# Two-layer graph network on one core: rows of A dealt over six attention strips, roots in three parts, Pool's first work in written order

## The chip, the cores and the metric

The kernel runs on one core of a Trainium2 chip. The core has a matrix engine (TensorE, "PE" in the profile; its weight loads are "PEld"), a vector engine (DVE), a scalar engine (ACT), a general engine (POOL) and a queue processor (SP) that mostly starts DMA transfers. Each engine works through its own list of instructions in order; semaphores make one wait for another. The metric is the time of the program on the device in microseconds, the median of several runs.

## The reference

x has 2708 rows (nodes) of 128 features, adj is a 2708 x 2708 matrix A of zeros and ones. Everything is fp32. Layer 0 adds three things to x and normalizes the rows:

```python
deg = clip(adj.sum(axis=1), 1.0)
dis = deg ** -0.5
diffusion = (dis[:, None] * adj * dis[None, :]) @ x - x
norms = maximum(norm(x, axis=-1), 1e-8)
sim = x @ x.T / (norms[:, None] * norms[None, :])
attn = softmax(beta * sim * adj, axis=1)
x = layernorm(x + diffusion + sigmoid(alpha) * (attn @ x - x))
```

Layer 1 multiplies x by a weight matrix, forms an attention from two scores per node, divides it by A times its exponentials, and multiplies by A again; its result is added to x and normalized. The change touches layer 0 only.

## The kernel before, in words

A is never kept whole on the chip. Its transpose is read in strips of 512 columns: six strips (the last has 148 columns), each of 22 blocks of 128 rows. Layer 0 has two stages.

**Attention** goes over the six strips in the order 2, 3, 4, 0, 1, 5; n counts this order from 0, and k counts the 22 blocks of a strip from 0. For each block, TensorE computes the similarities (`sim`, from the normalized and transposed rows `xn_t`, or by transposing a tile `turned` that an earlier strip has stored, since sim is symmetric). DVE multiplies them by a piece of A's transpose and by beta into `p_t` (and copies `sim` into `turned` where a later strip will need it). ACT takes the exponential of `p_t` in place, POOL adds it to `total`, and TensorE multiplies it with the rows of x into `att_acc`. Six buffers hold `p_t`, four PSUM tiles hold `sim`. After a strip, `attended` sums `total` by matmuls (`sums`), copies `att_acc` by ACT (`tr_sb`), transposes it (`tr_ps`) and adds it into `att`; this is written at k = 5 of the next strip. `att` starts as -sigmoid(alpha) * x.

**Preparing** the normalized rows runs within n = 0: squares and their sums (by DVE for the first two parts of the nodes, then by ACT), the power -1/2 on POOL (`norms`, tile `ss`), the scaling (`xn`, by DVE or ACT), and transposes by TensorE whose result is copied into `xn_t` (`turn_rows`, by ACT).

**Degrees**: the sum over a row of A. A block of 128 rows is loaded in two halves (`row`, 677 KB each, two buffers) by SP, and ACT adds each half up (an activation of 1354 columns with an accumulator, written to `deg2`). `roots` adds the halves, clips them and takes the power -1/2 on POOL (`dis`). In n = 5 the rows of x are multiplied by `dis` in place (L582), as soon as the attention has used them.

**Diffusion** (L703) then goes over strips 0 to 5 of A's transpose, loaded whole (`strip`, 5.8 MB in two halves, three homes in memory that pieces, stored tiles and other buffers of the attention must leave first): 22 blocks of two-pass matmuls for each, with the layer norm and the beginning of layer 1 for the strip before in between. `nat` are further loads of A by POOL's queue for layer 1.

**What sets the order.** SP's queue is one list: pieces of A's transpose (`load_piece`, five buffers), rows and strips stand in it one behind another, and a transfer whose buffer isn't free holds all that follow. For nearly all of n = 0, `strict` is set, and each PE, DVE and ACT instruction is pinned behind the one written before it on its engine (`pinned`). After that a planner orders the instructions by its own estimate of costs, within the dependences; a pin only says behind which instruction one must come. In the kernel before, POOL's instructions are not pinned, so that memsets written much later can come first, and the activations on `row` are pinned behind the last pinned ACT instruction only. The degrees are written from n = 1 on; the planner moves the last of them behind the end of n = 5.

The two steps that the change deals with, before it:

```python
if n > 0 and todo and (k % 6 == 5 if m < n else (k - 4 * n) % 3 == 1):
    degree(todo.pop(0))
if n == NS - 2 and k == NB - 1:
    while todo:
        degree(todo.pop(0))
```

Of the kernel before, what the change touches and what calls it, by code (L numbers as in the profile page):

```python
# [9 lines left out]
F32 = mybir.dt.float32  # L10
AF = mybir.ActivationFunctionType
ALU = mybir.AluOpType
AX = mybir.AxisListType
PSUM = bass.MemoryType.PSUM

P = 128
N = 2708
D = 128
NB = (N + P - 1) // P
# [3 lines left out]
NS = (N + SW - 1) // SW  # L23
# [7 lines left out]
Q = 256  # L31
# [8 lines left out]
TINY = 1e-18  # L40
# [4 lines left out]
def grouped(  # L45
# [14 lines left out]
    nc = tc.nc  # L60
# [13 lines left out]
    def blocks(s):  # L74
        return min(SW // P, NB - s * (SW // P))
# [10 lines left out]
    x_sb = lp.tile([P, NB, D], F32, name="x_sb")  # L86
    ident = const.tile([P, P], F32, name="ident")
# [3 lines left out]
    minus_half = const.tile([P, NB], F32, name="minus_half")  # L91
    nc.gpsimd.memset(minus_half, -0.5)
    plus_half = const.tile([P, 1], F32, name="plus_half")
# [10 lines left out]
    sig = const.tile([P, 1], F32, name="sig")  # L104
# [5 lines left out]
    def counted(name, pattern, base, step, size):  # L110
# [7 lines left out]
    node = counted("node", [[P, NB]], 0, 1, NB)  # L118
# [11 lines left out]
    pad = const.tile([P, NB], F32, name="pad")  # L130
    from_n = const.tile([P, NB], F32, name="from_n")
    after_node = const.tile([P, 2], F32, name="after_node")

    row0, row1, rest, head = (
        const.tile([P, 1], F32, name=n) for n in ("row0", "row1", "rest", "head")
    )

    four = const.tile([P, 32], F32, name="four")

    def constants():  # L140
        dve("tensor_scalar", pad, node, N - 0.5, 1e6, ALU.is_gt, ALU.mult)
        dve("tensor_scalar", from_n, node, float(-N), None, ALU.add)
        dve("tensor_scalar", after_node, node[:, 0:2], 1.0, None, ALU.add)
        dve("tensor_scalar", row0, node[:, 0:1], 0.0, None, ALU.is_equal)
        dve("tensor_scalar", row1, node[:, 0:1], 1.0, None, ALU.is_equal)
        dve("tensor_scalar", rest, node[:, 0:1], 1.5, None, ALU.is_gt)

        dve("tensor_scalar", head, node[:, 0:1], 1.5, TINY, ALU.is_lt, ALU.max)
        dve("tensor_reduce", four, ident.rearrange("p (q g) -> p g q", q=4), AX.X, ALU.add)

    deg2 = const.tile([P, NB, 2], F32, name="deg2")
    deg = const.tile([P, NB], F32, name="deg")
    dis = const.tile([P, NB], F32, name="dis")
    live = const.tile([P, NB], F32, name="live")

    cnt = const.tile([P, NS, 2, 2], F32, name="cnt")
    theta = const.tile([P, 2], F32, name="theta")
    ntheta = const.tile([P, 2], F32, name="ntheta")


    latest = {}

    def pinned(engine, op, *args, **kwargs):
        with ExitStack() as e:
            if engine in latest:
                e.enter_context(tc.issue_after(latest[engine].ins))
            latest[engine] = op(*args, **kwargs)  # L167

    strict = []

# [5 lines left out]

    def dve(op, *args, **kwargs):
        if strict:
            pinned("DVE", getattr(nc.vector, op), *args, **kwargs)
        else:  # L180
            getattr(nc.vector, op)(*args, **kwargs)  # L181

    def act(op, *args, **kwargs):
        if strict:
            pinned("ACT", getattr(nc.scalar, op), *args, **kwargs)
        else:
            getattr(nc.scalar, op)(*args, **kwargs)  # L187

    def over(t, m, n):
        return t.unsqueeze(2).to_broadcast([P, m, n])  # L190
# [81 lines left out]
    att = lp.tile([P, NB, D], F32, name="att")  # L272
# [3 lines left out]
    with ExitStack() as es:  # L276
        pa = pool("pa", stack=es)
# [4 lines left out]
        shift = pa.tile([P, 1], F32, name="shift")  # L282
# [40 lines left out]

        def norms(b0, b1):
            r = ss[:, b0:b1]
            nc.gpsimd.tensor_scalar(r, r, 1e-16, None, ALU.max)
            nc.gpsimd.tensor_tensor(r, r, minus_half[:, b0:b1], ALU.pow)

        def normalize(b0, b1):
            dve(  # L330
# [11 lines left out]
        def turn_rows(b0, b1, by):  # L342
            tp = ps_tp.tile([P, SW // P, P], F32, tag="tp", name="xn_ps")
            for b in range(b0, b1):
                mm(nc.tensor.transpose, tp[:, b - b0, :], xn(b, b + 1)[:, 0, :], ident)
            by(
                xn_t[:, b0 * P : b1 * P],
                tp[:, : b1 - b0, :].rearrange("p b i -> p (b i)"),
            )

        def by_act(o, i):
            act("copy", o, i)


        wa = pa.tile([P, 2], F32, name="wa")
        w_t = pa.tile([P, D], F32, name="w_t")
        spread = pa.tile([P, 1], F32, name="spread")
        up = pa.tile([P, 2], F32, name="up")
        down = pa.tile([P, 2], F32, name="down")
# [26 lines left out]
        squares(12, 16)  # L386
        norms(12, 16)

        def bounds():

            dve("tensor_tensor", up, up, down, ALU.subtract)
            nc.gpsimd.tensor_tensor(spread, spread, plus_half, ALU.pow)
            dve("tensor_scalar", spread, spread, 0.55, None, ALU.mult)
            dve("tensor_scalar", theta, up, spread, None, ALU.mult)
            for b, far, op in ((0, -100.0, ALU.is_lt), (1, 100.0, ALU.is_gt)):
                edge = pa.tile([P, 1], F32, name=f"edge{b}")
                lim = 0.5 if b == 0 else Q - 1.5
                dve("tensor_scalar", edge, node[:, b : b + 1], lim, far, op, ALU.mult)
                dve(
                    "tensor_tensor", theta[:, b : b + 1], theta[:, b : b + 1], edge,  # L400
                    ALU.add,
                )
            dve("tensor_scalar", ntheta, theta, -1.0, None, ALU.mult)

        def attention_starts():

            act("activation", sig, sig, AF.Exp, scale=-1.0)
            dve("tensor_scalar", sig, sig, 1.0, None, ALU.add)
            dve("reciprocal", sig, sig)
            dve("tensor_scalar", att, x_sb, sig, -1.0, ALU.mult, ALU.mult)  # L410

        def degree(ib):

            for h in range(2):
                z = pa.tile([P, N // 2], F32, tag="row", name="row", bufs=2)
                nc.sync.dma_start(z, adj[ts(ib, P), h * (N // 2) : (h + 1) * (N // 2)])
                pinned(
                    "ACT", nc.scalar.activation, z, z, AF.Copy,
                    accum_out=deg2[:, ib, h : h + 1],
                )  # L420

        def roots(b0, b1):

            t = deg[:, b0:b1]
            nc.vector.tensor_tensor(t, deg2[:, b0:b1, 0], deg2[:, b0:b1, 1], ALU.add)
            nc.vector.tensor_scalar(live[:, b0:b1], t, 0.0, None, ALU.is_gt)
            nc.vector.tensor_scalar(t, t, 1.0, None, ALU.max)
            nc.gpsimd.tensor_tensor(dis[:, b0:b1], t, minus_half[:, b0:b1], ALU.pow)

        def attended(s, acc, total):  # L430

# [18 lines left out]
        todo = list(range(NB))  # L450
        ended = None
        scaled = set()
        for n, s in enumerate(order):
            v, nb = width(s), blocks(s)
            acc = ps_acc.tile([P, SW], F32, tag="acc", name="att_acc")
            total = lp.tile([P, SW], F32, tag="total", name="total", bufs=2)
            nc.gpsimd.memset(total, 0.0)
            if v < nb * P:
                nc.gpsimd.memset(total[:, v : nb * P], 1.0)
            blocks_j = taken(n)  # L460

            prep = {
                (0, 1): lambda: normalize(12, 16),
                (0, 16): attention_starts,
                (0, 18): bounds,
                (0, 20): constants,
                (2, 14): lambda: roots(0, 6),
                (3, 16): lambda: roots(6, 12),
                (4, 17): lambda: roots(12, 18),
                (5, 2): lambda: roots(18, NB),  # L470
            }
            turns = {
                3: lambda: turn_rows(12, 16, by_act),
                7: lambda: (turn_rows(16, 20, by_act), turn_rows(20, 22, by_act)),
                13: lambda: turn_rows(0, 4, by_act),
                17: lambda: turn_rows(4, 8, by_act),
# [15 lines left out]
            place = {o: m for m, o in enumerate(order)}  # L492
            late_accs = []
            for k, jb in enumerate(blocks_j):
                if (n, k) in prep:
                    prep[n, k]()
                if n == 0 and k in turns:
                    turns[k]()
# [1 line left out]
                m = place[jb // 4]  # L500
# [7 lines left out]
                else:  # L508
# [2 lines left out]
                        xn_t[:, s * SW : s * SW + v], start=True, stop=True,  # L511
                    )
                p_t = pz.tile([P, SW], F32, tag="p", name="p_t")
                dve(
                    "scalar_tensor_tensor", p_t[:, :v], sim[:, :v], gentle,
                    pieces[s, jb // 4][:, jb % 4, :v], ALU.mult, ALU.mult,
                )
# [19 lines left out]
                r = valid(jb)  # L537

                def grown(p_t=p_t, r=r):
                    act("activation", p_t[:, :v], p_t[:, :v], AF.Exp, bias=shift)  # L540
                    nc.gpsimd.tensor_tensor(  # L541
                        total[:r, :v], total[:r, :v], p_t[:r, :v], ALU.add
                    )

                grown()
# [17 lines left out]
                if k == 5 and ended:  # L563
                    attended(*ended)
                    ended = None
                if n > 0 and todo and (k % 6 == 5 if m < n else (k - 4 * n) % 3 == 1):
                    degree(todo.pop(0))
                if n == NS - 2 and k == NB - 1:
                    while todo:
                        degree(todo.pop(0))  # L570
                if n == NS - 1 and k in (7, 13, 18, 21):

                    done = sorted(blocks_j[: k + 1 if k == NB - 1 else k - 1])
# [31 lines left out]
    e2_p = late.tile([P, NB], F32, name="e2_p")  # L605
    e2_w = late.tile([P, NB, 32], F32, name="e2_w")
    ct = late.tile([P, 4], F32, name="ct")
    nc.gpsimd.memset(e2_w, 0.0)
    nc.gpsimd.memset(x1[:, NB - 1, :], 0.0)

    tot = ps_tot.tile([P, 2, SW], F32, name="tot")
    early = KEPT * SW // 4
# [390 lines left out]
    def by_dve(o, i):  # L1003
        dve("tensor_copy", o, i)
# [691 lines left out]
```

## Time and profile before

| what | value |
|---|---|
| median of 3 runs | 762.48 us (762.22 to 765.44) |
| the profiled execution | 763.92 us |
| its span, first to last instruction | 762.0 us |
| busy: PE, DVE, ACT, POOL | 721.7, 453.2, 419.7, 259.1 us |
| start and n = 0 (0 to 60 us): PE busy | 51.41 us |
| 60 to 195 us (n = 1 to n = 4): PE busy | 133.45 of 135 us |
| 222 to 250 us: PE busy, granted clock | 22.75 of 28 us, 0.88 |
| 250 to 345 us (diffusion): PE busy | 95.00 of 95 us |
| row halves: issue to landing, min, median, max | 3.8, 5.8, 13.0 us |

The profile is of one execution. It lists each instruction's start and length, the idle time of its engine before it, and what ended that idle time (the releaser). L167, L175, L181 and L187 are lines of helpers that issue for PE, DVE and ACT, so a group is told by its tiles. The granted clock is the share of TensorE's full clock.

### The profile page before, as it was taken

The numbers are of one execution on the slowest core, as the hardware profiler recorded it, in microseconds if no ns is written. First come the engines' busy times: TensorE is split into PE (matmuls) and PEld (weight loads), VectorE is DVE, ScalarE is ACT, GpSimd is POOL, SyncE is SP. The second block draws the span as 40 slices with busy tenths as digits, with TensorE's granted clock in tenths as the row PEclk, the third lists the DMA queues.
The fourth block names the chain that finished last, engine by engine and source line by source line (L and its number), as shares of the span: only waits on it lengthen the run. The fifth ranks groups of instructions, "written<-read, shape, count | busy, mean of one in ns | idle before, by whom it ended". The sixth has DMA issues, their size and how long they took to land. (4 is left out here: it accounts for less than half of the span.)

```text
span 762.0 us, 7796 instructions
## 1 busy us (share of the span) xinstructions
PE 721.7 (95%) x2561; PEld 350.4 (46%) x2561; DVE 453.2 (59%) x947; ACT 419.7 (55%) x601; POOL 259.1 (34%) x255
## 2 busy tenths in 40 slices
PE   6989999999997999999898799999999999999995
PEld 4434454545553444445334344444444445544444
DVE  4786776664631443235895998998999982203032
ACT  4747777868551222112264599999999994001000
POOL 6857696979741000001124887111111000000000
PEclk9999999999998999999999999999999999999999
DMA  8738988898989996535369835964444430898970
GB/s 299 282 134 317 313 321 310 321 342 302 345 305 412 379 346 240 188 125 208 117 243 241 255 102 187 223 187 158 173 171 143 157 135 1 269 314 301 319 236 22
DMA packets 67522, 179.87 MB, mean 236 GB/s; under 512 B 4238, under 2 KB 18354, under 8 KB 64450
## 3 DMA queue, kind: packets, MB, share of 16 engines
q1 hardware_dynamic: 52996, 123.10, 45.7%
q0 software_dynamic: 8208, 53.30, 22.1%
q10 hardware_dynamic: 6270, 2.90, 1.3%
q8 instruction: 22, 0.36, 0.2%
q14 instruction: 26, 0.21, 0.1%
HBM read 176.44 MB, written 2.84 MB: 235 GB/s over the span
## 5 line engine op out<-in xcount | busy, mean ns | idle before, releaser
L541 POOL TENSOR_TENSOR total<-total,p_t 128x512 f32<-128x512 f32 (+2 forms) x132 | 152.4, 1155 | 44.5 <-ACT p_t L187 28.3
L167 PE MATMUL num<-ring,wt 128*128 128x512 f32 (+1 forms) x288 | 128.3, 545 | 7.5 <-DVE q L167 4.9
L167 PE MATMUL m_acc<-q,xws 128*128 128x512 f32 x240 | 120.5, 592 | 0.4 <-ACT q L167 0.4
L703 PE MATMUL dif_acc<-strip,x_sb 128*128 128x512 f32 (+1 forms) x264 | 107.7, 557 | 5.3 <-DVE x_sb L582 4.6
L181 DVE SCALAR_TENSOR_TENSOR p_t<-sim,gentle,piece 128x512 f32<-128x512 f32 (+1 forms) x111 | 71.3, 670 | 50.2 <-PE sim L175 35.9
L175 PE MATMUL att_acc<-p_t,x_sb 128*128 128x512 f32 (+1 forms) x228 | 97.2, 545 | 3.4 <-ACT p_t L187 3.1
L167 DVE COPY q<-num 128x512 f32<-128x512 f32 x144 | 86.4, 613 | 16.6 <-PE num L167 15.5
L1233 PE MATMUL h_acc<-ring,m_sb 128*128 128x512 f32 x220 | 95.7, 593 | 0.0
L187 ACT ACTIVATE p_t<-p_t,shift 128x512 f32<-128x512 f32 (+1 forms) x111 | 69.4, 656 | 31.4 <-DVE p_t L181 30.8
L167 PEld LDWEIGHTS num<-ring,wt 128*128 128x128 f32 x288 | 51.5, 190 | 67.4 <-issue 55.7
L167 DVE SCALAR_TENSOR_TENSOR q<-sr_b,nc_s,q 128x1536 f32<-128x1536 f32 (+1 forms) x48 | 77.4, 1613 | 1.2 <-ACT q L167 1.2
L167 ACT ACTIVATE q<-q,head,rest 128x1536 f32<-128x1536 f32 (+1 forms) x48 | 70.5, 1509 | 8.5 <-DVE ring L167 4.5
L703 PEld LDWEIGHTS dif_acc<-strip,x_sb 128*128 128x128 f32 x264 | 47.2, 194 | 56.0 <-issue 49.5
L167 PEld LDWEIGHTS m_acc<-q,xws 128*128 128x128 f32 x240 | 45.5, 190 | 57.1 <-issue 55.7
L954 POOL DMA_INDIRECT ring<-in_adj_t,k_no x24 | 33.5, 1397 | 108.0 <-PE num L167 103.1
L167 ACT ACTIVATE row<-row 128x1354 f32<-128x1354 f32 x44 | 58.3, 1324 | 17.6 <-DMA row<-in_adj 17.2
L1233 PEld LDWEIGHTS h_acc<-ring,m_sb 128*128 128x128 f32 x220 | 41.3, 190 | 49.3 <-issue 49.3
L167 ACT ACT_TABLE_LOAD x48 | 61.6, 1283 | 3.8 <-issue 2.9
L167 ACT ACTIVATE q<-q,c_s 128x1536 f32<-128x1536 f32 (+1 forms) x48 | 62.7, 1354 | 0.3
L175 PEld LDWEIGHTS att_acc<-p_t,x_sb 128*128 128x128 f32 x228 | 39.1, 190 | 49.6 <-ACT p_t L187 27.6
L1248 DVE TENSOR_TENSOR hh<-rows,x 128x512 f32<-128x512 f32 (+1 forms) x6 | 3.8, 641 | 85.2 <-PE rows L1171 82.5
L1243 ACT COPY ht<-h_acc 128x512 f32<-128x512 f32 (+1 forms) x6 | 3.2, 536 | 91.3 <-PE h_acc L1233 91.2
(270 smaller groups left out, 823.0 us busy)
## 6 DMA issues: line engine op xcount, KB each, us to landing
row<-in_adj SPq DMA_DIRECT2D x44, 677.0 KB, 5.8
strip<-in_adj_t SPq DMA_DIRECT2D x10, 2816.0 KB, 14.8
ring<-in_adj_t SPq DMA_DIRECT2D x27, 1024.0 KB, 5.0
piece<-in_adj_t SPq DMA_DIRECT2D x24, 1024.0 KB, 6.2
nat<-in_adj_t POOLq DMA_DIRECT2D x22, 768.0 KB
piece<-in_adj_t SPq DMA_DIRECT2D x7, 512.0 KB, 6.0
strip<-in_adj_t SPq DMA_DIRECT2D x2, 814.0 KB, 13.8
last<-in_adj_t POOLq DMA_DIRECT2D x1, 1628.0 KB
```

Of the source, the lines that this page charges most:

```text
L167: latest[engine] = op(*args, **kwargs)
L175: op(*args, **kwargs)
L181: getattr(nc.vector, op)(*args, **kwargs)
L187: getattr(nc.scalar, op)(*args, **kwargs)
L541: nc.gpsimd.tensor_tensor(total[:r, :v], total[:r, :v], p_t[:r, :v], ALU.add)
L703: nc.tensor.matmul(acc[:, :v], x_sb[:, jb, :], st[:, jb, :v], start=(jb == 0), stop=(jb == NB - 1),)
L954: nc.gpsimd.indirect_dma_start(out=ring[g % RING][P - G :, :], out_offset=None, in_=adj_t[:, :], in_offset=bass.IndirectOffsetOnAxis(ap=k_ ...
L1233: nc.tensor.matmul(acc[:, : h1 - h0], m_sb[:, kb + b, :], a[:, b, h0:h1], start=(kb + b == 0), stop=(kb + b == NB - 1),)
L1243: nc.scalar.copy(ht[:, h0:h1], acc[:, : h1 - h0])
L1248: nc.vector.tensor_tensor(hh[:, b0 : b0 + n, :], rows[:, :n, :], x1[:, ib + b0 : ib + b0 + n, :], ALU.add)
```

## The change

- **Degrees.** `rows_at` says at which k of which strip a block of rows is written: three in n = 0, six in n = 1, five in n = 2 and n = 3, three in n = 4, none in n = 5. Each is put in by `in_order`, which pins it behind the last `p_t` of DVE and the last exponential of ACT (`behind`).
- **Roots** come in three parts (blocks 0 to 8, 8 to 18, 18 to 22) instead of four, at n = 3, k = 2; n = 4, k = 1; n = 4, k = 14, and are pinned too. The last part was at n = 5, k = 2.
- **att** is started strip by strip (at k = 14 of n = 0, k = 4 of the others) instead of for all nodes at k = 16 of n = 0; the sigmoid moves to k = 12.
- **bounds and constants**, small DVE work, move from n = 0 into n = 1, in three parts each.
- **Pool** goes through the new helper `gps`, so that its work in n = 0 stands as written, and two memsets of layer 1 (`e2_w`, `x1`) are pinned behind its last pinned instruction.
- **The second part's transposes** (blocks 12 to 16) are copied into `xn_t` by DVE instead of ACT.

The diff, cut:

```diff
-    def constants():
+    def constants(part):
...
+    def gps(op, *args, **kwargs):
+        if strict:
+            pinned("POOL", getattr(nc.gpsimd, op), *args, **kwargs)
         else:
-            getattr(nc.scalar, op)(*args, **kwargs)
+            getattr(nc.gpsimd, op)(*args, **kwargs)
...
+        def by_dve(o, i):
+            dve("tensor_copy", o, i)
...
+        def attention_starts(s):
+            mine = slice(s * 4, s * 4 + blocks(s))
+            dve(
+                "tensor_scalar", att[:, mine, :], x_sb[:, mine, :], sig, -1.0, ALU.mult,
+                ALU.mult,
+            )
+
+        behind = {}
+
+        def in_order(f):
+
+            latest.update(behind)
+            strict.append("some")
+            f()
+            strict.pop()
...
-            nc.gpsimd.memset(total, 0.0)
+            gps("memset", total, 0.0)
...
-                (0, 16): attention_starts,
-                (0, 18): bounds,
-                (0, 20): constants,
-                (2, 14): lambda: roots(0, 6),
-                (3, 16): lambda: roots(6, 12),
-                (4, 17): lambda: roots(12, 18),
-                (5, 2): lambda: roots(18, NB),
+                (0, 12): alpha_starts,
+                (1, 7): lambda: bounds(0),
+                (1, 9): lambda: bounds(1),
+                (1, 11): lambda: bounds(2),
+                (1, 13): lambda: constants(0),
+                (1, 15): lambda: constants(1),
+                (1, 17): lambda: constants(2),
+                (3, 2): lambda: roots(0, 8),
+                (4, 1): lambda: roots(8, 18),
+                (4, 14): lambda: roots(18, NB),
+            }
+
+            rows_at = {
+                0: (13, 16, 19), 1: (5, 8, 11, 14, 17, 20), 2: (4, 9, 12, 15, 18),
+                3: (4, 9, 13, 16, 19), 4: (3, 6, 9), 5: (),
             }
             turns = {
-                3: lambda: turn_rows(12, 16, by_act),
+                3: lambda: turn_rows(12, 16, by_dve),
...
-                if n > 0 and todo and (k % 6 == 5 if m < n else (k - 4 * n) % 3 == 1):
-                    degree(todo.pop(0))
-                if n == NS - 2 and k == NB - 1:
-                    while todo:
-                        degree(todo.pop(0))
+                if n > 0 and (n, k) in prep:
+                    in_order(prep[n, k])
+                if k == (14 if n == 0 else 4):
+                    in_order(lambda: attention_starts(s))
+                if k in rows_at[n]:
+                    in_order(lambda: degree(todo.pop(0)))
...
-    nc.gpsimd.memset(e2_w, 0.0)
-    nc.gpsimd.memset(x1[:, NB - 1, :], 0.0)
+    pinned("POOL", nc.gpsimd.memset, e2_w, 0.0)
+    pinned("POOL", nc.gpsimd.memset, x1[:, NB - 1, :], 0.0)
```

## The prediction

> **What bounds the kernel now.** I read the page's slices first, then TensorE's timeline over the first 250 us, then, wherever TensorE stood, the engine it stood for. TensorE is busy 721.7 of the 762.0 us of the span, so only its idle or slowed time can be won. The change touches the first 230 us. The slices (19 us each):
>
> ```profile
> PE   6989999999997999999898799999999999999995
> PEclk9999999999998999999999999999999999999999
> DMA  8738988898989996535369835964444430898970
> ```
>
> PE's first three digits are the start and strip n=0; the 7 in the thirteenth slice (229 to 248 us) comes with the lowest clock of the page. That place by stretches of 5 us (length; busy time of PE, weight loads, DVE, ACT, POOL; granted clock; DMA share; GB/s):
>
> ```profile
> 225.00:230.00 5.00, 4.33 (x16) 2.17 (x15) 0.92 (x4) 0.00 (x0) 0.00 (x0) 1.00 1.02 419
> 230.00:235.00 5.00, 2.70 (x6) 0.91 (x6) 0.49 (x4) 2.79 (x4) 0.00 (x0) 1.00 1.04 407
> 235.00:240.00 5.00, 2.72 (x3) 1.18 (x4) 1.40 (x3) 0.00 (x0) 2.14 (x3) 0.63 1.05 408
> 240.00:245.00 5.00, 5.00 (x10) 2.13 (x9) 0.00 (x0) 0.00 (x0) 0.00 (x0) 0.69 1.03 425
> ```
>
> The timelines of PE, ACT and POOL say who waited for whom (start, length, engine, line; in brackets the idle time before it and its releaser):
>
> ```profile
> 229.86 2.84 PE L703 MATMUL dif_acc<-strip,x_sb 128*128 128x512 f32 x6 [0.68 <-DMA strip<-in_adj_t]
> 231.71 1.33 ACT L167 ACTIVATE row<-row 128x1354 f32<-128x1354 f32 x1 [8.83 <-DMA row<-in_adj]
> 235.20 1.03 POOL L428 TENSOR_TENSOR dis<-deg,minus_half 128x4 f32<-128x4 f32 x1 [12.58 <-DVE deg L427]
> 237.28 10.86 PE L703 MATMUL dif_acc<-strip,x_sb 128*128 128x512 f32 x18 [4.58 <-DVE x_sb L582]
> ```
>
> The last two row halves of A land at 231.7, so the last degrees, their roots and the scaling of x_sb (L582) are late, and the diffusion of strip 0 stops at its fifteenth block for 4.58 us. SP's timeline shows why they land late: they are issued at 218.35, behind half a strip, on a DMA that is full (share above 1).
>
> ```profile
> 192.60 0.50 SPq L691 DMA_DIRECT2D strip<-in_adj_t  x1
> 215.00 0.46 SPq L691 DMA_DIRECT2D strip<-in_adj_t  x1
> 218.35 2.31 SPq L416 DMA_DIRECT2D row<-in_adj  x2
> 220.84 72.78 SPq L691 DMA_DIRECT2D strip<-in_adj_t  x10
> ```
>
> The stalls of the first strip (timelines of POOL, PE and DVE):
>
> ```profile
> 5.98 0.69 POOL L608 MEMSET e_w<- 128x704 f32 x1
> 17.97 1.35 POOL L327 TENSOR_TENSOR ss<-ss,minus_half 128x6 f32<-128x6 f32 x1
> 17.10 1.13 PE L167 MATMUL sim<-xn_t 128*128 128x512 f32 x2 [1.29 <-ACT xn_t L167]
> 41.26 2.04 DVE L167 TENSOR_SCALAR att<-x_sb,sig 128x2816 f32<-128x2816 f32 x1 [0.37 <-DVE sig L167]
> 45.25 1.12 PE L167 MATMUL sim<-xn_t 128*128 128x512 f32 x2 [1.72 <-ACT xn_t L167]
> ```
>
> **The change part by part.** Sums are against the profiled span, 762.0 us (that execution took 763.92).
>
> *Rows earlier, roots (18, NB) in n=4: the stall goes.* In the built order SP issues the last two row halves before the last two pieces, and ACT takes them after the third and fifth p_t of n=5 (before: after the last). The scaling of the last blocks then waits for nothing but its attention matmuls. Removed from PE's queue: 4.58 us; the 0.68 us for strip 0's second half; and the slow clock. For the clock, 18 matmuls took 10.86 us where full speed takes 18 x 0.43 = 7.7 (0.86 us per pair, as at 222.40: 14 in 6.17): 3.1 us. [...] Together 8.4 us.
>
> *What is late next: the strips.* Strip 0's first half loses its place at 192.6: both halves now stand behind the last piece, whose buffer comes free with the fourth p_t of n=5, about 205 (DVE did those at 203.7 to 205.4). Halves of 2.88 MB at the 0.41 MB/us of the rows above take 7.0 us each, so with 2 us of start-up they land near 214 and 221. Diffusion starts near 220 (below) and needs the second half 11 x 0.86 = 9.5 us later. Strip 1 (5.8 MB), nat (2.4) and strip 5 (1.7) follow until 221 + 9.9 / 0.41 = 245; strip 1, ahead of strip 5 in SP's queue, lands by about 240 and its first half, first needed near 239, by 234 even when shared with nat. Cost 0, with some 5 us of cover. From there PE was 95.00 of 95 us busy (250 to 345), so the gain passes on.
>
> *n=5 without diffusion between its matmuls.* Before, 3.5 us of diffusion (218.1 to 219.9, 220.2 to 221.9) filled PE there; in the new order none, and the row sums (sums, 2 matmuls) stand ahead of diffusion in PE's queue and wait for Pool. Pool in n=5: 22 additions of 0.53 us, and now the root (1.04) and the memsets of e2_w and x1 (0.69 + 0.20) among them: 13.8 us against 14 us of PE work. Pool's idle time of before in n=5 (4.95 us) was ACT's waiting; bounds 0 and 2.5 us of waiting for Pool, I take 1.2. ACT has two row halves there instead of six, which gives back about half of PE's 0.63 + 0.58 us of idle in 195 to 200 and 210 to 215: -0.5. Diffusion's start: attention's end of before, 222.6, less the 3.5, -0.2 (below), -0.5, +1.2, and 0.5 for the sums: 220.1.
>
> *Start: Pool in written order.* The memset of e2_w no longer stands between norm and power: -0.66 us to the first sim. But both memsets of total (0.53 each) now follow the second norm and push the first addition from 12.70 to about 13.0.
>
> *Second part's transposes by DVE.* The copy runs on DVE at 14.0 to 14.7, after the third p_t, instead of ACT at 16.48, and PE's 1.29 us goes: sim of k = 4 at 15.0 instead of 17.1. It does not last: ACT's normalizing of blocks 16 to 21 waits for Pool's power, 17.97 + 1.35 before, and Pool (second power to 12.0, memsets, three additions) reaches its end at about 19.2 again, at best 18.7. So at k = 7 the gain of both edits is -0.5 (bounds 0 and -1.3).
>
> *Three degrees in n=0.* ACT now has two row halves (1.32 + 0.19 us each) after the p_t of k = 13, 16 and 19 (k from 0; before, two near the strip's end). With two row buffers, the second pair is issued when ACT has finished the first: p_t 13 ends at 36.1, the rows at 37.5 and 39.0; issue 37.7, landing 5.8 us later (median of 44; 3.8 to 13.0) at 43.5, less with the DMA share of 0.43 here: 42.8. ACT takes them until 45.8, then copies xn_t, which the sim of k = 18 waits for: 46.3 instead of 45.25, and instead of 42.9 with nothing in the way: a stall of 3.4 us. Queued behind it on ACT are all later p_t, and PE's matmuls behind those. The third pair lands near 49 and 50.5, and ACT is done with it at 53.5; p_t 20 and 21 end at 54.8 and the strip at 56.0. Before it ended at 56.2, since DVE then spent 2.04 us on att, 2.3 on bounds and 1.0 on constants between p_t, and ACT took two row halves at the same place. Net with the start: -0.2 (bounds -1.5 and +3.5). [...]
>
> *att by strips, bounds and constants in n=1, roots in three parts.* The same work in DVE's gaps, 88 us busy of 135 between 60 and 195: 0. Theta's 1.25 us against 0.14 for its neighbours is waiting for Pool; six slices of att could each wait for one addition (1.28), spread over six strips. Cover: PE 133.45 of 135 busy. n=1 to n=4 have 36 row halves on ACT in both orders, a buffer's two uses mostly 4 to 6 p_t apart in both: 0, between -1.5 and +1.5. Spread's power (0.55 on Pool) moves to the end of n=0: 0.
>
> Sum: -8.4 + 1.2 - 0.5 - 0.2 = -7.9 us; span 754.1. On the median shown, 762.48 - 7.9 = 754.6.
>
> **Rivals.** 0.5% is about what a measurement of this kernel can tell from no change: under 758.7 is faster, over 766.3 slower.
> - *Forecast, 754.6* (own range 751.5 to 758.5). For: the chain row, degree, root, x_sb is plain, and nothing after 250 us stands in the way.
> - *The clock falls in n=0, or DVE holds p_t of n=5 for the last degree* (deg now stands among them and waits for ACT's last row half): -7.9 + 3.1 + 1.5 = -3.3, 759.2. [...] Against: the low DMA share shortens the landing.
> - *The stall only changes its place: strip 0 comes late.* If SP is held at the last piece until t, PE waits t + 9 - 220, and the clock falls too: at t = 215.8 the gain is gone, 762.5. Against: nothing but DVE's fourth p_t and ACT's rows of n=4 holds it.
> - *Slower: landing of the rows in n=0.* Each us beyond 5.1 at p_t 16 stops ACT, so PE, and delays the third pair's issue too: about 2 us for one, and 3.1 of clock. At 7.5 us of landing the 7.9 are gone (2 x 2.4 + 3.1), from 9.4 us on it is slower by 0.5%; at 10.5, 2 x 5.4 + 3.1 - 7.9 = +6.0, 768.5. The 13.0 us happened with the DMA full, which it is not here.
>
> **How the numbers follow.** Forecast 0.62, second 0.20, strip 0 late 0.11, slower 0.07. The time is the first's. Leaving out the slower case and part of its neighbour above, and the far end below, the range is 751.0 to 761.5. Faster: 0.62 and some of the second, with 0.1 of it that falls under 758.7: 0.72; same 0.20; slower 0.08.
>
> **What would show it.** Right: no wait of PE for x_sb L582 near 230; the last row on ACT before 213; PE's clock 1.00 from 220 to 250; strip 0's diffusion ending near 239 instead of 247; strips still 22.6 us apart after it. In n=0: the sim of k = 4 near 15.0, a stall before that of k = 18 of 2.5 to 4 us with ACT waiting for row's DMA, and the strip's last attention matmul near 56. Wrong: a clock under 1 at 40 to 55, PE waiting for strip by DMA, or sums waiting for Pool by more than 2.5 us.

## The result, and the profile after

The changed kernel takes 761.1 us (median of 20 runs, 758.39 to 772.14); the kernel before, run beside it, 762.43 (20 runs, 757.36 to 769.06). The ratio is 0.9993, 95% interval 0.9972 to 1.0014: no change that can be measured, where 754.6 was forecast. The profiled execution of the changed kernel was the longest of its 20 (772.14 us); up to the end of diffusion (358.1 us in both) it keeps pace with the profile before. What it has more lies behind that, where the change does nothing; the greater part is one wait of PE for a transfer of layer 1:

```profile
474.21 2.05 PE L173 MATMUL num<-ring,wt 128*128 128x512 f32 x2 [8.82 <-DMA ring<-in_adj_t,k_no]
```

The comparison below is therefore of the first 250 us, and a second trace of the same kernel (e1) stands beside it.

The slices of the page of the changed kernel (19.3 us each):

```profile
PE   8989999999999999999998895999999999999995
PEclk9999999999979999999999997999999999999998
```

The 7 of PE before 250 us is gone. A low digit of the clock has come in the twelfth slice, 212 to 231 us. By stages (busy time of PE, weight loads, DVE, ACT, POOL; granted clock; DMA share; GB/s):

```profile
0.00:60.00 60.00, 53.26 (x146) 27.03 (x147) 34.48 (x61) 37.39 (x89) 37.95 (x49) 0.97 0.81 284
60.00:195.00 135.00, 131.86 (x444) 66.55 (x442) 92.87 (x162) 100.48 (x151) 107.84 (x87) 1.00 0.87 306
195.00:222.00 27.00, 26.61 (x100) 17.06 (x99) 14.06 (x36) 17.12 (x34) 20.45 (x29) 0.81 0.98 331
222.00:250.00 28.00, 26.76 (x86) 13.84 (x85) 6.20 (x19) 4.55 (x9) 5.63 (x10) 1.00 0.97 361
250.00:345.00 95.00, 95.00 (x301) 42.84 (x303) 36.51 (x172) 16.48 (x24) 3.58 (x10) 1.00 0.67 245
```

From 222 to 250 PE is busy for 26.76 us at full clock; before it was 22.75 at 0.88. So the stall at 230 is really gone, and with it the slow clock behind it. But 0 to 60 has fallen from 1.00 to 0.97, and n=5 (195 to 222) from 1.00 to 0.81. Four points of the schedule show the account, each read as the start of ACT's copy of a finished accumulator to tr_sb, in us of the trace:

| kernel | n=0 ends | n=4 ends | n=5 ends | strip 0's diffusion ends |
|---|---|---|---|---|
| before | 56.35 | 202.99 | 222.60 | 247.32 |
| changed | 58.66 | 207.00 | 227.09 | 247.07 |
| changed, second trace (e1) | 59.16 | 206.61 | 223.69 | 246.97 |
| e2, two rows in n=0 | 52.02 | 204.93 | 218.42 | 243.07 |
| e3, wide sums | 57.71 | 205.05 | 221.21 | 240.10 |
| e5, sums behind | 57.97 | 205.10 | 221.87 | 240.75 |
| e6, e2's rows and sums behind | 52.26 | 205.79 | 222.13 | 241.01 |
| e7, before with earlier rows | 56.21 | 205.80 | 224.97 | 246.18 |
| e8, dummies in n=0 | 56.66 | 204.38 | 221.24 | 244.54 |
| e9, e6 with wide sums | 51.98 | 204.20 | 217.84 | 237.70 |

Before, 3.86 us of strip 0's diffusion (1.98 + 1.88) lay inside n=5. With these taken off n=5 and put to the last stretch, the lengths before are 56.35, 146.64, 15.75 and 28.58 us. The changed kernel's are 58.66, 148.34, 20.09 and 19.98. So the last stretch gives 8.6 us, very near the 8.4 costed, and 2.3, 1.7 and 4.3 are lost ahead of it: the gain was made and spent in the same 250 us. (For n=1 to n=4, the 1.7, no run gives a cause.)

**Where the 2.3 of n=0 went.** Timelines of PE and ACT of the changed kernel:

```profile
42.91 1.02 PE L173 MATMUL att_acc<-p_t,x_sb 128*128 128x512 f32 x2
46.99 1.13 PE L173 MATMUL sim<-xn_t 128*128 128x512 f32 x2 [3.06 <-ACT xn_t L173]
47.96 1.81 PE L173 MATMUL att_acc<-p_t,x_sb 128*128 128x512 f32 x2
42.44 1.32 ACT L173 ACTIVATE row<-row 128x1354 f32<-128x1354 f32 x1
45.05 1.33 ACT L173 ACTIVATE row<-row 128x1354 f32<-128x1354 f32 x1 [1.20 <-DMA row<-in_adj]
46.38 0.56 ACT L173 COPY xn_t<-xn_ps 128x512 f32<-128x512 f32 x1
```

ACT waits for the second pair of row halves with the copy of xn_t queued behind them, PE stands 3.06 us, and what follows runs slow (1.81 us where 1.02 is usual). From this sim to the end of n=0 the four traces with one stretch of 3.41 us at half clock here take 11.62 to 11.67 us (the changed kernel, e1, e3, e5); e8, where the clock stays full, takes 9.97. So the clock costs 1.7 us here. The rest comes of the start. The first sim was at 9.79 us before; with Pool in written order it is at 8.98 to 9.37 in e2 to e6, e8 and e9, as forecast, but at 10.45 in both traces of the changed kernel (and e10). Matmuls on ones at the start (`idle_ps`) show why, in the changed kernel and then in e5:

```profile
6.87 2.06 PE L173 MATMUL idle_ps<-ones 128*128 128x256 f32 x4
6.66 1.11 PE L173 MATMUL idle_ps<-ones 128*128 128x256 f32 x4
```

The first run at about half speed, though the clock column shows 1.00 there; e5's instructions up to this place are the same, so it is not the order of the work. Why both traces of the changed kernel have it, and those seven not, is open. The clock around the two places, in stretches laid to where it changes (same columns as above):

```profile
44.64:48.05 3.41, 1.05 (x3) 0.58 (x4) 0.00 (x0) 2.52 (x4) 0.34 (x1) 1.00 0.90 282
48.05:51.46 3.41, 3.41 (x6) 1.35 (x5) 1.35 (x2) 0.72 (x1) 2.19 (x2) 0.50 1.01 409
51.46:54.87 3.41, 3.41 (x10) 1.50 (x9) 2.70 (x4) 2.50 (x4) 1.29 (x1) 1.00 0.07 25
208.48:211.89 3.41, 3.41 (x23) 2.71 (x23) 2.31 (x10) 3.39 (x7) 1.33 (x3) 1.00 0.93 289
211.89:215.30 3.41, 3.41 (x14) 2.77 (x14) 1.53 (x7) 1.31 (x4) 2.04 (x4) 0.50 1.04 384
215.30:218.71 3.41, 3.41 (x14) 2.48 (x14) 2.29 (x8) 1.81 (x5) 2.75 (x5) 0.50 1.05 407
218.71:222.13 3.42, 3.42 (x15) 2.75 (x13) 1.77 (x4) 0.85 (x3) 3.03 (x6) 0.50 1.05 407
222.13:225.54 3.41, 3.23 (x21) 2.50 (x20) 2.26 (x5) 1.65 (x4) 2.47 (x5) 1.00 0.84 326
```

The clock column shows 0.50 for one stretch of 3.41 us in n=0 (48.05 to 51.46) and for 10.24 us in n=5 (211.89 to 222.13), and 1.00 in the other rows. The stretch before the first fall holds 1.05 us of PE work. The stretch before the second is full by the PE column, so it must be read by what it was full of (the last two lines are from the end of n=5):

```profile
207.65 1.08 PE L182 MATMUL sim<-ident,turned 20*128 20x20 f32 x5
208.66 1.05 PE L467 MATMUL sums<-ones,total 128*128 128x1 f32 x8
209.58 0.63 PE L182 MATMUL tr_ps<-ident,tr_sb 128*128 128x128 f32 x4
210.05 1.71 PE L182 MATMUL sim<-ident,turned 128*128 128x128 f32 x8
211.68 0.69 PE L182 MATMUL att_acc<-p_t,x_sb 128*128 128x148 f32 x2
...
226.23 0.83 PE L182 MATMUL att_acc<-p_t,x_sb 128*128 128x148 f32 x4 [0.87 <-ACT p_t L192]
227.43 0.60 PE L467 MATMUL sums<-ones,total 128*128 128x1 f32 x4 [0.38 <-POOL total L198]
```

For 4.03 us (207.65 to 211.68) PE does transposes and one-column sums only. A count of the columns that PE writes, transposes like the rest (a 128x512 record counts 512, a 20x20 one 20, one of sums 1, one cut by an edge its share), gives about 1,240 for the stretch from 208.48, where one full of 512-column records (229.0 to 232.4) has about 4,060. That PE work was short ahead of both falls, idle at the first and small at the second, is what this trace shows; that the clock fell for it is theory A below, and e8 and e9 try it, each in one of the two places.

### The profile page after: what moved, and what is told of

It reads as the page before. It is cut to its first block, busy times and chain, and to the rows that moved or that the text cites. A ratio compares the mean times of both kernels' runs of the same rounds, so it can differ in the third digit from the quotient of the medians.

```text
span 770.2 us, 7806 instructions
## 1 busy us (share of the span) xinstructions
PE 728.9 (95%) x2561; PEld 357.1 (46%) x2561; DVE 452.7 (59%) x950; ACT 419.0 (54%) x600; POOL 258.6 (34%) x254
## 5 line engine op out<-in xcount | busy, mean ns | idle before, releaser
L173 PE MATMUL num<-ring,wt 128*128 128x512 f32 (+1 forms) x288 | 131.2, 555 | 14.4 <-DMA ring<-in_adj_t,k_no 10.2
L198 POOL TENSOR_TENSOR total<-total,p_t 128x512 f32<-128x512 f32 (+3 forms) x111 | 126.0, 1136 | 33.8 <-ACT p_t L192 28.5
L746 PE MATMUL dif_acc<-strip,x_sb 128*128 128x512 f32 (+1 forms) x264 | 104.1, 544 | 0.0
L182 PE MATMUL att_acc<-p_t,x_sb 128*128 128x512 f32 (+1 forms) x228 | 98.8, 560 | 3.8 <-ACT p_t L192 3.5
L182 PEld LDWEIGHTS att_acc<-p_t,x_sb 128*128 128x128 f32 x228 | 41.8, 204 | 45.7 <-issue 22.5
```

Source lines behind the costliest of these rows:

```text
L198: getattr(nc.gpsimd, op)(*args, **kwargs)
L746: nc.tensor.matmul(acc[:, :v], x_sb[:, jb, :], st[:, jb, :v], start=(jb == 0), stop=(jb == NB - 1),)
```

## The experiments

Two theories and a third. A: the gain was lost at half clock, behind the stall in n=0 and in n=5. B: it was lost in order and waits (rows on ACT, Pool's lag), with the clock as a trifle. C: strip 0's transfer sets when diffusion can start, so nothing ahead of it counts. All ratios are to the kernel before on the same chip.

**e1: the changed kernel again.**

> The changed kernel once more, for a second trace. Theory A (clock): the 8.4 us won at 230 to 245 were lost again in half-clock windows of 3.41 us, behind the stall before sim of k = 18 in n=0 and behind the 4.03 us of transposes and one-column sums at 207.65 to 211.68 in n=5; such windows lie differently to the work in each execution, so this trace may show fewer of them there, each 1.7 us, and strip 0's diffusion then ends at 242 to 247. Theory B (order and waits): it ends at 246 to 248 whatever the clock does. Theory C (strip 0's transfer sets the start of diffusion): PE waits for strip in this trace. Median 760 to 763 in all three.

761.4 us (22 runs), ratio 0.9988 (0.9966 to 1.001). The second trace has full clock where the first was slow in n=5 (195 to 222 at 1.00; the 3.41 us from 208.76, in the same work, have about 1,830 columns), and yet strip 0 ends at 246.97. Timelines of PE, POOL, ACT and DVE:

```profile
222.83 0.83 PE L182 MATMUL att_acc<-p_t,x_sb 128*128 128x148 f32 x4 [1.02 <-ACT p_t L192]
225.66 0.88 PE L467 MATMUL sums<-ones,total 128*128 128x1 f32 x4 [2.00 <-POOL total L198]
212.05 2.83 POOL L198 TENSOR_TENSOR total<-total,p_t 128x148 f32<-128x148 f32 x4 [1.09 <-ACT p_t L192]
214.99 1.02 POOL L173 TENSOR_TENSOR dis<-deg,minus_half 128x4 f32<-128x4 f32 x1
215.96 0.68 POOL L173 MEMSET e_w<- 128x704 f32 x1
216.75 8.85 POOL L198 TENSOR_TENSOR total<-total,p_t 128x148 f32<-128x148 f32 x13
210.18 1.33 ACT L173 ACTIVATE row<-row 128x1354 f32<-128x1354 f32 x1
213.25 1.28 DVE L625 TENSOR_TENSOR x_sb<-x_sb,dis 128x768 f32<-128x768 f32 x1
215.33 0.72 PE L182 MATMUL sim<-ident,turned 128*128 128x128 f32 x3 [1.09 <-DVE p_t L187]
```

Pool is the chain here: it waits for p_t behind the last row half on ACT, does the root and two memsets (one shown), and then needs 8.85 us for 13 additions, 0.68 each on the mean: nine take 0.50 with 0.08 between, and four that fall beside a scaling of x_sb by DVE take 0.69 to 1.09. PE has finished attention at 223.66 and stands until 225.66, with diffusion queued behind the sums; its data and x_sb are ready, and nothing in this trace waits for strip, so C falls. And half clock lies behind that wait, for 3.41 us:

```profile
222.41:225.82 3.41, 0.99 (x6) 0.76 (x6) 1.33 (x3) 0.95 (x3) 3.10 (x6) 1.00 1.03 387
225.82:229.23 3.41, 3.41 (x8) 1.86 (x9) 0.40 (x2) 0.00 (x0) 1.63 (x3) 0.50 1.06 394
229.23:232.64 3.41, 3.41 (x10) 1.50 (x9) 0.00 (x0) 0.00 (x0) 0.00 (x0) 1.00 1.03 403
```

So A and B each have a part, and they hide each other: where half clock slows PE in n=5, Pool catches up and sums wait 0.38 us; where the clock is full, they wait 2.00 and the 3.41 us behind are slow. That both traces end strip 0 within 0.1 us of each other is chance: the terms differ.

**e2: two degrees in n=0 instead of three.**

```diff
-                0: (13, 16, 19), 1: (5, 8, 11, 14, 17, 20), 2: (4, 9, 12, 15, 18),
+                0: (13, 19), 1: (5, 8, 11, 14, 17, 20), 2: (3, 6, 9, 12, 15, 18),
```

> Two degrees in n=0 (after the p_t of k = 13 and 19) instead of three, six in n=2 instead of five. A: the stall of 3.06 us before sim of k = 18 goes, with the half-clock window behind it where one falls: -3 to -5 us, ratio to the kernel before 0.993 to 0.996. B: -3.0 us, 0.995. C: n=0 ends 3 us earlier, but diffusion starts no earlier: 0.999.

761.55 us (22 runs), ratio 0.9976 (0.995 to 1.0002). In the trace the stall is gone, n=0 ends at 52.02 instead of 57.7 to 59.2, and strip 0 at 243.07: 4 us earlier. Sums wait 2.30 us for Pool, and half clock (219.2 to 226.0) lies about that wait. The time does not show those 4 us: its interval reaches from -3.8 us to +0.2, so this run alone is inconclusive. The trace tells where its own execution (761.4 us) lost them: diffusion ends at 354.1 us instead of 358.1, and in layer 1 PE then waits for a transfer:

```profile
463.94 1.10 PE L173 MATMUL num<-ring,wt 128*128 128x512 f32 x2 [3.46 <-DMA ring<-in_adj_t,k_no]
```

The traces of the changed kernel, e3 and e10 have such a wait too (8.82, 5.46 and 4.59 us), the others none above 2.3. So behind the place of the change the time varies by as much as the gains that are sought. Much of the gain in n=0 is given back by n=4's end (202.99 before, 204.93 here), but there the built order has already drawn work of n=5 forward, as the shorter n=5 shows.

**e3: more work for PE.**

```diff
+            m = P if s == order[NS - 2] else 1
...
-                    sums[:, b, 0:1], total[:, ts(b, P)], ones[:, 0:1], start=True, stop=True
+                    sums[:, b, :m], total[:, ts(b, P)], ones[:, :m], start=True, stop=True
```

> Only the four row-sum matmuls of n=4, which run in n=5, are made 128 columns wide instead of one (the same numbers, only more of them): work is added to PE, 4 x about 0.2 us, and the stretch without a full matmul falls from 4.03 us to under 2.5. A: no half clock from 205 to 228, -3 us (one to three windows of 1.7 less 0.8), ratio to the kernel before 0.994 to 0.997. B and C: +0.5 us or nothing, 0.999 to 1.000.

757.34 us (22 runs), ratio 0.9942 (0.9918 to 0.9967), what A expected. The clock is 1.00 from 205 to 250, and strip 0 ends at 240.10. But this is not shown to be A's doing, for the edit moved more than was meant: with other costs, the planner set the row sums of n=5 behind the diffusion of strip 0, where Pool's lag costs nothing. e5 takes that part alone.

**e4: e2 and e3 together.**

> Both edits: two degrees in n=0, and the row sums of n=4 128 columns wide. A: -6 to -8 us, ratio to the kernel before 0.989 to 0.992, diffusion of strip 0 ending near 240. B: -2.5, 0.996. C: 0.999.

758.73 us (22 runs), ratio 0.9968 (0.9947 to 0.9989). A's -6 to -8 is wrong. In this built order the sums of n=5 stand ahead of diffusion again: they wait 2.29 us for Pool, the clock is at half from 219.6 to 226.3, and strip 0 ends at 243.03, as in e2. So most of e3's lead in the trace was the place of those sums.

**e5: only the place of the sums.**

```diff
-                nc.tensor.matmul(
-                    sums[:, b, 0:1], total[:, ts(b, P)], ones[:, 0:1], start=True, stop=True
+                mm(
+                    nc.tensor.matmul, sums[:, b, 0:1], total[:, ts(b, P)], ones[:, 0:1], start=True, stop=True
...
-            nc.tensor.matmul(
+            latest["PE"] = nc.tensor.matmul(
...
         if s == 0:
+            strict.append("behind")
             attended(*ended)
+            strict.pop()
```

> The changed kernel with one edit: the row sums of n=5 (and the transposes after them) are kept behind the 22 diffusion matmuls of strip 0 on PE. Theory P (Pool's lag is what was paid): in the second trace of the changed kernel sums waited 2.00 us for Pool's last addition, stood 0.7 us ahead of diffusion, and a half-clock window of 3.41 us followed the wait (1.7 us); all of it goes, diffusion of strip 0 takes 19.05 us for its 44 matmuls and ends at 241.5 to 243.5, -4 us, ratio to the kernel before 0.992 to 0.995. Theory W (the gain of the wide sums came from the transposes' stretch in n=5 alone): -0.7 us at most, ratio 0.998.

758.85 us (14 runs), ratio 0.9956 (0.993 to 0.9983). PE's timeline:

```profile
221.00 0.83 PE L182 MATMUL att_acc<-p_t,x_sb 128*128 128x148 f32 x4 [1.03 <-ACT p_t L192]
221.67 19.05 PE L746 MATMUL dif_acc<-strip,x_sb 128*128 128x512 f32 x44
240.55 0.50 PE L173 MATMUL sums<-ones,total 128*128 128x1 f32 x4
```

The 22 diffusion matmuls (44 records of 0.43 us) run in one piece of 19.05 us with nothing between, and strip 0 ends 6.2 us earlier than in e1, 4.4 of it behind the end of n=5 (18.88 us against 23.28). P holds by the trace; the interval of the time just takes in W's 0.998 too.

**e6: sums behind, two degrees in n=0, memsets in n=1.** e2's and e5's edits, and:

```diff
                 (1, 17): lambda: constants(2),
+                (1, 19): lambda: (
+                    gps("memset", e2_w, 0.0), gps("memset", x1[:, NB - 1, :], 0.0)
+                ),
...
-    pinned("POOL", nc.gpsimd.memset, e2_w, 0.0)
-    pinned("POOL", nc.gpsimd.memset, x1[:, NB - 1, :], 0.0)
...
```

> Sums behind strip 0's diffusion, two degrees in n=0 instead of three (six in n=2), and Pool's memsets of e2_w and x1 in n=1 instead of among n=5's additions. P together with the stall of n=0 (3.06 us and a window of 1.7): diffusion of strip 0 ends at 236 to 239, ratio to the kernel before 0.987 to 0.991 (752 to 755 us). Rival D (layer 1 is set by its own transfers, and gives back what comes early): strip 0 ends as early, but the ratio is 0.996 or more.

755.36 us (6 runs), ratio 0.9891 (0.985 to 0.9933). Strip 0 ends at 241.01, not at 236 to 239: the trace has half clock in n=5, from 203.0 to 213.2, behind transposes and the one-column sums of n=4. The time follows the trace here (-6.3 us at strip 0, -6.9 in the median), so rival D, that layer 1 always gives the gain back, falls.

**e7: the kernel before with only earlier rows and roots.**

```diff
-                (5, 2): lambda: roots(18, NB),
+                (4, 20): lambda: roots(18, NB),
+            }
+            rows_at = {
+                0: (), 1: (2, 5, 8, 11, 14, 17, 20), 2: (3, 6, 9, 12, 15, 18, 21),
+                3: (5, 8, 11, 13, 16, 19), 4: (3, 6), 5: (),
             }
...
-                if n > 0 and todo and (k % 6 == 5 if m < n else (k - 4 * n) % 3 == 1):
+                if k in rows_at[n]:
...
```

> The kernel before with only this: degrees closer together in n=1 to n=4 (7, 7, 6 and 2), none in n=5, and the roots of blocks 18 to 21 in n=4. If the earlier rows alone bring Pool's lag to the front (no diffusion before n=5's row sums): the 4.58 us stall goes, sums wait 1 to 2.5 us for Pool, strip 0 ends at 241 to 245, ratio 0.993 to 0.998. If the wait comes of the other edits (Pool in written order, memsets among the additions): no wait, strip 0 ends near 239, ratio 0.988 to 0.990.

761.53 us (22 runs), ratio 0.9986 (0.996 to 1.0012): no gain that can be measured, less than was expected. PE's timeline:

```profile
224.11 0.83 PE L175 MATMUL att_acc<-p_t,x_sb 128*128 128x148 f32 x4 [1.50 <-ACT p_t L187]
226.37 0.61 PE L435 MATMUL sums<-ones,total 128*128 128x1 f32 x4 [1.43 <-POOL total L545]
227.09 3.17 PE L704 MATMUL dif_acc<-strip,x_sb 128*128 128x512 f32 x7
```

The stall of 4.58 is gone and a wait of 1.43 for Pool has come, as expected if the earlier rows alone bring the lag to the front: no memset or written order of Pool is in this kernel. Strip 0's end (246.18) was expected at 241 to 245; n=5 had half clock as well, from 207.6 to 214.4 and from 217.8 to 221.2.

**e8: dummy matmuls in the stall of n=0.**

```diff
+                if n == 0 and k == 18:
+                    idle2_ps = ps_mm.tile([P, SW], F32, tag="mm", name="idle2_ps")
+                    for _ in range(7):
+                        mm(
+                            nc.tensor.matmul, idle2_ps[:, : 2 * P], ones,
+                            ones.unsqueeze(1).to_broadcast([P, 2, P]),
+                            start=True, stop=True,
+                        )
```

> The changed kernel with seven dummy matmuls (ones by ones, 128x256, into a PSUM tile that nothing reads) put on PE ahead of the sim of k = 18 in n=0, where it waits 3.06 to 3.35 us for ACT; nothing else moves. Theory A (PE's clock halves after a window of 3.41 us with little matmul work in it): full clock from 40 to 60, n=0 ends 1.5 us earlier, median -1 to -2 us against the changed kernel, though only work was added. Rival (the clock falls for another reason, such as the wait itself or the load of the DMA): half clock at 46 to 52 as in all three traces, 0 to +0.5 us.

758.86 us (22 runs), ratio 0.9955 (0.9932 to 0.9977); the changed kernel was at 0.9988 (0.9966 to 1.001). PE's timeline, and then the stretches of 4 us around the place:

```profile
42.33 3.18 PE L173 MATMUL idle_ps<-ones 128*128 128x256 f32 x14
46.69 1.12 PE L173 MATMUL sim<-xn_t 128*128 128x512 f32 x2 [1.18 <-ACT xn_t L173]
```

```profile
44.00:48.00 4.00, 2.83 (x11) 1.66 (x10) 0.09 (x1) 2.52 (x4) 0.60 (x1) 1.00 1.00 372
48.00:52.00 4.00, 4.00 (x11) 1.76 (x10) 3.25 (x5) 2.29 (x3) 2.65 (x3) 1.00 0.58 228
```

The sim starts at 46.69, among the 46.09 to 47.50 of the changed kernel, e1, e3 and e5, which stall here without dummies; the DMA is as full, and the clock stays at 1.00. From this sim to the end of n=0 it is 9.97 us, against 11.62 to 11.67 in those four: 1.7 us, half of the 3.41 us at half clock. So it is PE's lack of work that brings the slow clock here, not the late copy or the full DMA. Useless work made this place faster; the ratios of the whole agree, though their intervals still touch. In n=5 this trace again has sums waiting 2.01 us for Pool, with half clock behind from 223.7 to 227.1.

**e9: e6 with e3's wide sums.**

> The fastest kernel so far (sums behind strip 0's diffusion, two degrees in n=0, memsets in n=1), and the row sums of n=4 128 columns wide. Its trace had half clock for 10.2 us from 203 to 213, behind transposes and one-column sums. Theory A (the clock follows the matmul work of a window of 3.41 us): the wide sums keep it at 1.00, strip 0's diffusion ends at 236 to 238 instead of 241, median 752 to 754. Rival (the clock in n=5 only slows work that Pool and ACT bound anyway): strip 0 ends at 240.5 to 241.5, median 755 to 756.

753.12 us (6 runs), ratio 0.9883 (0.9841 to 0.9925). As A expected, the half clock of 203 to 213 is gone (1.00 from 195 to 215): the stretch of 3.41 us that in e6, from 199.55, has about 1,670 columns has 2,870 here. One stretch at half clock has come at 216.2 behind waits for p_t (1.37 and 0.52 us), and strip 0 ends at 237.70:

```profile
217.59 20.07 PE L748 MATMUL dif_acc<-strip,x_sb 128*128 128x512 f32 x44
237.50 0.50 PE L173 MATMUL sums<-ones,total 128*128 128x1 f32 x4
```

In the time, widening the sums is not shown by any one pair: by the ratios it is worth 0.0014 between e5 and e3, 0.0008 between e2 and e4, 0.0008 between e6 and e9, 0.6 to 1.1 us, each far inside its interval, though all three have one sign. This version beats both kernels.

**e10: ACT copies the second part's transposes again.** `turn_rows(12, 16, by_act)` in place of `by_dve`.

> The changed kernel with one part undone: the copy of the second part's transposes is ACT's again. If the part is worth what was costed, PE waits some 1.3 us for xn_t before the sim of k = 4, but the sim at k = 7 starts within 0.5 us of the changed kernel's, since ACT's normalizing waits for Pool's power in both. If it is worth more, n=0 ends 1 us or more later (against 58 to 59).

One execution (775.11 us), read only at the start, which runs alike in e1 (first sim at 10.45 in both). PE waits 0.82 us for xn_t before a sim at 18.08 (at 17.13 in e1), and the transposes of k = 7 start at 23.33 against 22.28: DVE's copy is worth 1.05 us there, about twice what was costed for it and Pool's order together. n=0 ends at 62.11, after a stall of 4.28 us and with half clock from 48.3 to 55.1.

**e11: dummies in the stall of the kernel before.** Ten dummies are pinned between the fourteenth and the fifteenth block of strip 0:

```diff
+            if s == 0 and jb == 14:
+                latest["PE"] = last
+                for _ in range(10):
+                    pinned(
+                        "PE", nc.tensor.matmul, tot[:, 1, : 2 * P], ones,
+                        ones.unsqueeze(1).to_broadcast([P, 2, P]),
+                        start=True, stop=True,
+                    )
...
```

> The kernel before with ten dummy matmuls (ones by ones, 128x256, into a PSUM tile that is written afresh later) on PE in the stall of 4.58 us ahead of the fifteenth diffusion block of strip 0; nothing else moves, and the stall's cause stays. Theory A: the clock stays 1.00 through 236 to 243, strip 0's diffusion ends near 244 instead of 247.3, median -1.7 to -3.4 us, ratio 0.9955 to 0.998. Rival (the clock follows the wait or the full DMA, not PE's work): half clock as before, 0 to +0.5 us, ratio 1.000.

```profile
234.40 4.48 PE L167 MATMUL tot<-ones 128*128 128x256 f32 x20
240.02 7.99 PE L714 MATMUL dif_acc<-strip,x_sb 128*128 128x512 f32 x18 [1.15 <-DVE x_sb L582]
```

The 18 records behind the stall take 7.99 us instead of 10.86, 2.9 less, at clock 1.00: the term of 3.1 in the forecast was rightly sized. The time is 761.67 us (22 runs), ratio 0.9995 (0.9973 to 1.0017), that is between -2.1 and +1.3 us: the gain seen in this place does not show in the whole, and why is not settled. (The trace itself lost 2.4 us ahead of the place, 1.2 of them in n=0, with half clock from 8.6 to 15.4 us.)

## Why the prediction was wrong, step by step

In short: the 8.4 was won. What failed is that everything ahead of it was costed at full clock, in n=0 and in n=5, and that Pool's lag and the degrees in n=5 were put too low. The terms of the sum against the second trace, where n=5 ran at full clock (lengths from the table):

| step | forecast | measured |
|---|---|---|
| stall at 230, strip wait, slow clock | -8.4 | -9.0 (the last stretch 28.58 before, 23.28 here, less the 3.7 of the next row) |
| sums wait for Pool | +1.2 | +2.0, and +1.7 for the 3.41 us at half clock behind it |
| n=5 with fewer rows on ACT | -0.5 | +1.3 |
| start and n=0 | -0.2 | +2.8, of it +1.7 for 3.41 us at half clock |
| n=1 to n=4 | 0 | +0.8 |
| sum | -7.9 | -0.4 (strip 0 ends at 246.97 instead of 247.32) |

- *Rows earlier: the stall goes.* Right. Nothing waits for x_sb near 230, the last row half on ACT is at 210.45 (forecast: before 213), the clock is 1.00 from 222.1 to 250 in the first trace, and the strips that follow are still 22.7 to 22.8 us apart. SP issues strip 0 at 208.86, a few us later than worked out, and its halves land 12.2 and 18.7 us after their issue, where 9 and 16 were estimated (the 2 us of start-up in that are what the shortest row half before leaves: 3.8 us, less 1.7 for 677 KB at 0.41 MB/us). It is in time: the rival of a late strip 0 is out.
- *"n=5 without diffusion between its matmuls."* This is the step that failed most. Its mechanism was named (the sums stand ahead of diffusion and wait for Pool), and the bound of 2.5 held for the wait: 2.00, 2.01, 2.30, 2.29. Two things were missing. First, half clock lies about the wait: 3.41 us of it in e1 (+1.7) and e8, 6.8 in e2 and e4. Second, without diffusion n=5 has stretches of small work (208.48 to 211.89: about 1,240 columns); the work was costed by its durations at full clock, and I read a busy PE as a PE that keeps its clock (10.24 us at half clock in the first trace). Pool's work was sized by 0.53 us per addition, without the 0.08 between two; the 13 in a row took 0.68 each.
- *-0.5 for fewer rows on ACT in n=5.* Wrong in sign. Two row halves still fell there, at its start, and held p_t from Pool (1.09 us and more); then DVE did the last degree and the first scaling of x_sb (1.28 us) among the p_t, and PE waited 1.09 us for the p_t behind it and 1.02 for a later one, behind another scaling (1.14 us). The second rival had put 1.5 us on just this.
- *Three degrees in n=0.* The chain was right to a fraction: stall forecast 3.4, measured 3.06 to 3.68; second pair on ACT until 45.8, measured 46.4. In e3 and e5 n=0 ends at 57.7 and 58.0, which less the 1.7 of the half clock is the 56.0 forecast. The sum has nothing for the clock here, and that was wrong: it fell in each of the five traces that have this stall unfilled, for 3.41 us in four of them (the changed kernel, e1, e3, e5), for 6.8 in e10. In the kernel before, the clock had stayed at 1.00 from 40 to 50, through 1.72 us of idling; that was no measure for 3 us. The 3.1 that the second rival has for the clock was too much for this place: it is the loss of the row of 237.28 to 248.14, with 6.83 us at half clock (2.40 of its first 3.41 us busy), and 1.7 was measured here. The rest of the +2.8 is in the main the slow start, which no step of the prediction dealt with and whose cause is open.
- *Pool in written order.* Right where the start is not slow: first sim 0.4 to 0.8 us earlier, -0.66 forecast, and the sim of k = 4 at 14.94 to 15.22 (15.0 forecast).
- *Second part's transposes by DVE.* Right in direction, undersized: 1.05 us at k = 7 (e10).
- *n=1 to n=4.* 0, between -1.5 and +1.5, was costed; +0.8 and +1.7 in the two traces. Why is open.

What happened was nearest in form to the second rival (-3.3 us: slow clock in n=0, DVE holding p_t), which lacked the same thing: a price for the half clock behind Pool's wait.

## What to carry to other kernels

When a stall is taken out, ask what stands ahead of the next bound work in the in-order queue: here two tiny matmuls that no one needed yet held 19 us of ready work. And read TensorE by its work and its clock, not by the busy column alone: in the first trace 3.41 us full of transposes and one-column sums (about 1,240 columns) had 10.24 us at half clock behind them, and a wait of 3.06 us had 3.41. Here dummies in that wait (e8) and wider sums (e9 against e6) kept the clock of their place at 1.00; elsewhere it is a thing to try, not a rule. Then judge such a gain first in its place: here the draw of waits and half clock elsewhere was as large as the gains sought.

## What was not expected of the hardware

- The clock column shows 0.50 for 3.41 us in n=0 of the changed kernel (48.05 to 51.46), for 10.24 us in its n=5 (211.89 to 222.13), and for 6.83 us in the kernel before (236.27 to 243.10).
- In the 3.41 us ahead of such a fall PE had 0.00 us of work (before, 232.86), 0.99 (e1, 222.41), 1.05 (n=0, 44.64), or 3.41 of small work (208.48, about 1,240 columns). And in n=5 it was busy for the whole 10.24 us at half clock.
- Where the half clock lies differs from execution to execution: the mean granted clock of the changed kernel's 20 runs goes from 0.976 to 0.991, by estimate 14 to 37 us at half clock ((1 - clock) x 2 x span). A single trace therefore shows one draw: the same stretch of transposes was followed by half clock in the first trace of the changed kernel, and by full clock in e1.
- Additions of Pool that take 0.50 us took 0.69 to 1.09 beside a scaling of x_sb by DVE (e1, 216.75 to 225.60), and 1.25 and 0.96 in the first trace (at 219.94 and 224.78).
